# An attention and feed-forward block on one core: the front in written order, idle matmuls ahead of it, and the weights' check moved to SP's queue

## The chip, the cores and the metric

The kernel runs on one core of a Trainium2 chip. The metric is the device time of the whole kernel in microseconds (us); lower is better. Before the change the median of three runs is 1353.18 us.

The engines by the names of the profile: PE (TensorE, matmuls), DVE (VectorE), ACT (ScalarE), POOL (GpSimd) and SP (SyncE, which here only issues DMAs). ACT and POOL issue DMAs too.

## What is computed

The inputs are x of 4 x 1024 x 256 and weights. In short:

```python
x = x + layernorm(attention(layernorm(x), Wqkv, Wout))   # 16 heads of 16
x = x + layernorm(ffn(layernorm(x)))
# attention: softmax(q k^T / 4) v, then @ Wout.T
#            softmax is exp(x - max) / (sum + 1e-6)
# ffn:  h = silu(x w1 * s1) * (x w2 * s2)
#       h = gelu(h h1 * t1);  h = gelu(h h2 * t2);  h w3 * s3
```

The feed-forward weights are ternary in these inputs. The kernel computes with them in a rounded format, and counts on the chip whether any weight changes by the rounding (a second condition bounds the scores). Only if a count is not zero does a slow general branch run; with these inputs it doesn't.

## The kernel before

**Attention.** The four batches (`b`) have 16 heads in four groups of four (`g`), and the 1024 queries are taken in two halves (`h`). A *unit* is one (b, g, h), 32 in all, in that order. In a unit, eight chunks of 128 keys and two pairs of heads make 16 *tiles*. Per tile, `exponentials` (lines 434 to 442) makes two score matmuls into one of three PSUM buffers `s` and one exponential on ACT, 128 x 1024, into a ring of eight tiles; `weigh` (444) makes four matmuls into the accumulator `acc`, of which there is one; `rise` (451) takes maxima on DVE (`top`). At the end of a unit, `unit_end` (583) copies `acc` to `o` on DVE and adds the division to the side work.

**Group operands.** Scores are made from `stacks`, in which four parts (high and low of keys and queries) lie below one another. `stack(b, g)` (409) fills them by 32 DMAs from the projected `cq` tiles, all on SP's queue. There are two sets, used by groups in turn; `unit_end` of the second half of group g issues the `stack` of group g + 2, or of the next batch.

**Side work.** The loop of lines 841 to 861 makes three tiles in a turn and ends a turn with `side.take()` (553). That runs the steps of several chains which are due: a step has a gap, counted in turns from the step before it in its chain, or from the turn in which the chain was added. Only one step with tensor work is taken in a turn. Projections for the next batch, V, the division, the output projection, the layer norms and the score bound (`flags`) run this way.

**The weights' check.** `check_weights` (227) makes four steps for one of 22 blocks of 512 KB: `load` the block from memory to `w`, `cast` it on POOL to the rounded `wr`, and twice `count` on DVE, which compares half a block; the second count also stores `wr` back to memory, from where the feed-forward stage loads its weights. The tiles `w` and `wr` have one buffer each. In before, the load and the store are issued by POOL, and all 22 blocks are one chain in the side work (830), a block in five turns.

**The front.** What stands ahead of line 808 is ordered by a scheduler; within `tc.manual_schedule()` (808) every engine issues in the order in which the code is written. In the front, x of batch 0 is loaded by SP in four DMAs, the query and key weights (`slotted`, 1 MB) by ACT in one DMA, from which POOL copies `wqk_sb`. Then, half by half: layer norm on DVE with a power on POOL (`rstd`), transposes on PE, key and query projections (310) with a copy on ACT and a low part on DVE, and 16 copies per projection for group 0, alternately on SP and POOL. Two of the four V steps (300) precede the first scores; the other two are side work.

Of the kernel before, what the change touches and what calls it, by code (L numbers as in the profile page):

```python
# [9 lines left out]
F32 = mybir.dt.float32  # L10
# [8 lines left out]
P = 128  # L19
HEADS = 16  # L20
DH = 16
SLOT = 32
# [4 lines left out]
RING = 8  # L27
TURN = 3
# [2 lines left out]
SAFE = 25.0  # L31
FULL = 32.0
EARLY = 256
SPREAD = 32.0
NQ = 512
WIDE = 1024
# [77 lines left out]
def tile_fast(ctx: ExitStack, tc: tile.TileContext, x, wqk, wv, wo, w1, w1s, w2, w2s, h1, h1s, h2, h2s, w3, w3s, out, bad):  # L114
# [22 lines left out]
        t, n = NH + (TPQ - 1) * h, TPQ * h  # L137
        return (slice(n, n + 1), view[:, h : h + 1, :]), (slice(n + 1, n + TPQ), view[:, t : t + TPQ - 1, :])

    def load_x(b):  # L140
        view = x[b].rearrange("(t p) d -> p t d", p=P)
        for h in range(NH):
            for at, tokens in pieces(h, view):
                nc.sync.dma_start(out=xs[b][:, at, :], in_=tokens)

    load_x(0)
    ident = const.tile([P, P], F32, name="ident")
    make_identity(nc, ident)
    ones = const.tile([P, 1], F32, name="ones")
# [16 lines left out]
        nc.sync.dma_start(out=scales[name], in_=w)  # L166
    w3s_sb = const.tile([P, D], F32, name="w3s_sb")
    nc.sync.dma_start(out=w3s_sb, in_=w3s.partition_broadcast(P))


    keep = ctx.enter_context(tc.tile_pool(name="keep", bufs=1))
# [6 lines left out]
    with ExitStack() as actx, ExitStack() as rctx:  # L178
# [4 lines left out]
        wo_sb = aw.tile([P, DC, D], F32, name="wo_sb")  # L183
        with tc.tile_pool(name="load", bufs=1, side="right") as load:
            slotted = load.tile([P, DC, 2, HEADS, SLOT], F32, name="slotted")
            nc.scalar.dma_start(out=slotted, in_=wqk.rearrange("(c p) (k h s) -> p c k h s", p=P, k=2, s=SLOT))
            for c in range(DC):
                nc.gpsimd.tensor_copy(wqk_sb[:, c], slotted[:, c, :, :, 0:DH])
        nc.scalar.dma_start(out=wv_sb, in_=wv.rearrange("(c p) d -> p c d", p=P))

        def load_wo(c):
# [35 lines left out]
        def check_weights(n, c):  # L227

            k = blocks.index((n, c))
            st = {}  # L230

            def rows(w):
                return w[c * P : (c + rows_at_once[n]) * P, :].rearrange("(i p) d -> p i d", p=P)

            def load():
                st["w"] = work.tile([P, WIDE], F32, tag="w", name="w", bufs=1)
                nc.gpsimd.dma_start(out=st["w"].rearrange("p (i d) -> p i d", i=rows_at_once[n]), in_=rows(weights[n]))

            def cast():
                st["r"] = work.tile([P, WIDE], F32R, tag="wr", name="wr", bufs=1)  # L240
                nc.gpsimd.tensor_copy(st["r"], st["w"])

            def count(j):
                def run():
                    w, r = (t[:, NQ * j : NQ * (j + 1)] for t in (st["w"], st["r"]))
                    i = k * (WIDE // NQ) + j
                    nc.vector.scalar_tensor_tensor(w, w, 1.0, r.bitcast(F32), ALU.mult, ALU.not_equal, accum_out=misses[:, i : i + 1])
                    if NQ * (j + 1) == WIDE:
                        nc.gpsimd.dma_start(out=rows(rounded[n]).bitcast(F32), in_=st["r"].bitcast(F32).rearrange("p (i d) -> p i d", i=rows_at_once[n]))

                return run

            return [Step(load, 0, False), Step(cast, 3, False)] + [Step(count(j), 1, False) for j in range(WIDE // NQ)]

        def to_scalar(o, i, scale=1.0):
            nc.scalar.activation(o, i, AF.Copy, scale=scale)  # L256
# [137 lines left out]
        def copies(g, w, c0=0, c1=S):  # L394

            m, i = g // GPT, g % 2

            def copy(u, j, n):
                def run(queue):
                    k = "hi" if (j // 2 == 0 if w == 0 else j % 2 == 0) else "lo"  # L400
                    r = (g % GPT) * HPG * DH + (2 * u + n) * DH
                    o = n * ROWS + j * DH
                    queue.dma_start(out=stacks[w, i, u][o : o + DH, c0:c1].bitcast(F32), in_=cq[w, m, k][r : r + DH, c0:c1].bitcast(F32))

                return run

            return [copy(u, j, n) for u in range(2) for j in range(PARTS) for n in range(2)]
# [7 lines left out]
        def slots(b, g, t0=0, t1=NT):  # L415


            def run():
                nc.gpsimd.tensor_copy(
                    vaug[g % 2][:, t0:t1, :, 0:DH], cv[:, t0:t1, HPG * DH * g : HPG * DH * (g + 1)].rearrange("p t (h e) -> p t h e", e=DH)  # L420
                )
                slotted[g % 2] = b, g, t1

            return run
# [143 lines left out]
                    self.take()  # L568

        side = Side()  # L570
        accs, tops, ends, later = {}, {}, {}, {}

        def begin(b):

# [8 lines left out]
        def unit_end(b, g, h):  # L583

            o = both.tile([P, NQ], F32, tag="o", name="o", bufs=2)
            to_vector(o, accs[b, g, h])

            assert g or not b or not any(step.tensor for step in ends[b - 1, h][0])
            unit = side.add(divide(g, h, o, tops[b, g, h]), True)
            if g == NG - 1:  # L590
                unit[0].extend(ending(b, h, to_scalar if (b, h) == (B - 1, NH - 1) else to_vector))
                ends[b, h] = unit
            if h < NH - 1:
                return

            n, at = g + 2, b
            if n >= NG:
                n, at = n - NG, b + 1
            if b == B - 1 and g == NG - 2:
                load_weights("h1", range(HC // 2))  # L600
            if at < B:
                if at > b:
                    assert not later["chain"][0]
                stack(at, n)
                slots(at, n)()
            if g == NG - 3 and b + 1 < B:
                v, qk1 = later["rest"]
                assert not later["chain"][0]
                later["chain"][0].extend(v)
                side.add([Step(lambda: None, 5, False)] + qk1)  # L610
            elif g == NG - 3:
                side.add([Step(lambda n=n: load_weights(n), 1, False) for n in ("w1", "w2", "w3")])
                side.add([Step(lambda: None, 7, False)] + prepare(0, to_vector))
            if g == NG - 1:
                begin(b + 1)
# [189 lines left out]
                chain = side.add(finish(n, ffn["a"]), True)  # L805
            side.flush()

        with tc.manual_schedule():
            norm, xt, qk, v, flags = prologue(0, lambda n: ps.tile([P, 2, NQ], F32, tag="big", name=n)[:, 0, :], to_scalar)
            queues = [nc.sync, nc.gpsimd]  # L810
            for h in range(NH):
                for step in norm[h]:
                    step.run()
            for h in range(NH):
                for step in xt[h]:
                    step.run()
                for w, step in zip((1, 0), qk[0][h]):
                    step.run()
                    for i, copy in enumerate(copies(0, w, h * NQ, (h + 1) * NQ)):
                        copy(queues[i % len(queues)])  # L820
            stacked[0] = 0, 0
            for step in v[: len(v) // 2]:
                step.run()
            slots(0, 0, 0, NT // 2)()
            stack(0, 1)
            for c in range(DC):
                load_wo(c)
            side.add(v[len(v) // 2 :] + [Step(slots(0, 0), 0, False), Step(slots(0, 1), 0, False)] + sum(qk[1], []) + [Step(lambda: side.add(flags), 0, False)])
            begin(0)
            side.add([s for k in blocks for s in check_weights(*k)])  # L830
            made = seen = weighed = 0

            def make(end):

                nonlocal made
                for k in range(made, min(end, len(tiles))):
                    assert k - weighed < RING
                    exponentials(k)
                    made = k + 1

            while weighed < len(tiles):
                n = made
                make(n + TURN - side.borrowed)
                if made == len(tiles):
                    n = made
                for k in range(seen, n - 1, 2):
                    rise(k)
                    seen += 2
                while weighed + 2 <= n:
                    b, g, h, c, _ = tiles[weighed]  # L850
                    if c == 0:
                        accs[b, g, h] = ps_acc.tile([P, NQ], F32, tag="acc", name="acc")
                    weigh(weighed, accs[b, g, h])
                    weighed += 2
                    if c == NT - 1:
                        unit_end(b, g, h)
                        if n < len(tiles):
                            break
                make(n + TURN)
                if weighed < len(tiles):  # L860
                    side.take()

            load_weights("h1", range(HC // 2, HC))
            rctx.close()
            ffn["a"] = halves(ctx.enter_context(tc.tile_pool(name="fa", bufs=1, reuse_waits="tile")), "ha")
            feed_forward()


@with_exitstack
# [233 lines left out]
```

## Time and profile before

| what | value |
|---|---|
| median of three runs | 1353.18 us (1352.37 to 1354.74) |
| the profiled execution: its time, its span | 1352.66 us, 1350.9 us |
| mean granted TensorE clock | 0.991 |
| PE first works at | 12.33 us |
| first scores, first exponential at | 31.16 us, 31.75 us |
| one copy of `stack` on SP | 0.59 us issue, 2.3 us to landing |
| load of a weight block from POOL | 4.2 us to landing |
| cast of a block on POOL, half a count on DVE | 1.04 us, 0.68 us |

The span runs from the first to the last instruction that the profiler saw. A row of a timeline gives the start, the duration, the engine and line, the operation, output and input, and in brackets how long the engine was idle before it and what released it. An engine with a q (SPq) is that engine's instruction queue, as when it issues a DMA. The attention stage lasts to about 680 us; the feed-forward stage follows.

### The profile page before, as it was taken

To read this page: it belongs to the slowest core of one execution; us is meant where nothing else is said; L and a number is where in the kernel's file an instruction comes from. 1 tells how busy PE (TensorE), PEld (TensorE's weight loads), DVE (VectorE), ACT (ScalarE), POOL (GpSimd) and SP (SyncE) were. 2 spreads that over 40 slices of the span, in tenths; PEclk is the share of its full clock that TensorE was granted. 3 is DMA by queue.
4 is the path that set the end of the run, shared out by engine and by line. 5 is a ranking of instruction groups with operands and counts; after the bars stand their busy time and mean duration, and the time that the engine had idled before them with its cause. 6 is when DMAs were issued, how large, how long until landed. Compare 5 with 4: busy or idle time off the path is not lost.

```text
span 1350.9 us, 18751 instructions
## 1 busy us (share of the span) xinstructions
PE 1273.3 (94%) x7034; PEld 799.0 (59%) x7034; DVE 732.5 (54%) x1553; ACT 684.1 (51%) x820; POOL 159.7 (12%) x200
## 2 busy tenths in 40 slices
PE   5989999899899999989999999999999999999995
PEld 3333434343343433333478888888888888888884
DVE  3466568755697565735573452725436364363533
ACT  2677787676777678888842231413224141231410
POOL 6241133210421012000000000000000000000000
PEclk9989999899999999999999999999999999999998
DMA  7554344542445432336130000000000000000000
GB/s 215 130 113 110 80 111 91 141 103 60 129 108 133 94 51 48 50 65 195 54 134 1 1 16 0 17 1 0 16 1 16 0 14 3 0 16 0 17 0 19
DMA packets 38390, 79.62 MB, mean 59 GB/s; under 512 B 11280, under 2 KB 21136, under 8 KB 38288
## 3 DMA queue, kind: packets, MB, share of 16 engines
q1 hardware_dynamic: 30384, 52.88, 18.1%
q0 software_dynamic: 7360, 24.12, 5.3%
q10 hardware_dynamic: 544, 1.31, 0.3%
q8 instruction: 58, 0.95, 0.3%
q14 instruction: 44, 0.36, 0.1%
HBM read 28.98 MB, written 15.73 MB: 33 GB/s over the span
## 4 chain that ended last, share of the span: by engine, by line
PE 76%; DVE 12%; ACT 7%; issue 2%; POOL 1%; DMA 1%; SPq 1%; ACTq 0%; POOLq 0%; DVEq 0%
PE ph L686 35%; PE acc L449 13%; PE s L441 8%; ACT e L442 5%; PE p L314 5%; PE pz L739 4%; PE pg L686 3%; PE py L506 2%; PE pv L305 2%; DVE top L458 2%; DVE sg L702 2%; PE po L470 1%; DVE st L92 1%; DVE ha_lo L691 1%; DVE o L259 1%
## 5 line engine op out<-in xcount | busy, mean ns | idle before, releaser
L442 ACT ACTIVATE e<-s 128x1024 f32<-128x1024 f32 x512 | 484.9, 1032 | 143.4 <-PE s L441 128.0
L449 PE MATMUL acc<-e,vaug 128*32 128x512 f32 x2048 | 258.0, 607 | 0.1
L722 ACT ACTIVATE a<-ph,h_scale 128x512 f32<-128x512 f32 x128 | 81.0, 685 | 307.3 <-PE ph L686 307.3
L441 PE MATMUL s<-sq,sk 64*128 64x512 f32 x1024 | 195.9, 452 | 28.0 <-ACT e L442 20.3
L686 PE MATMUL ph<-hb_lo,h 128*128 128x512 f32 x512 | 199.7, 390 | 0.0
L686 PE MATMUL ph<-hb_hi,h 128*128 128x512 f32 x512 | 199.6, 390 | 0.0
L441 PEld LDWEIGHTS s<-sq,sk 64*128 64x128 f32 x1024 | 87.5, 185 | 164.5 <-ACT e L442 121.0
L458 DVE TENSOR_TENSOR top<-top,e 128x512 f32<-128x512 f32 x192 | 146.4, 762 | 29.7 <-ACT e L442 23.4
L102 POOL TENSOR_TENSOR rstd<-ve,minus_half 128x4 f32<-128x4 f32 (+1 forms) x33 | 37.1, 1125 | 772.5 <-DVE ve L100 772.5
L723 DVE CAST ha_hi<-a 128x512 fp32r<-128x512 f32 x64 | 27.1, 424 | 158.2 <-ACT a L722 158.2
L449 PEld LDWEIGHTS acc<-e,vaug 128*32 128x32 f32 x2048 | 49.7, 109 | 106.1 <-issue 96.7
L686 PEld LDWEIGHTS ph<-hb_hi,h 128*128 128x128 f32 x512 | 96.2, 188 | 20.1
L686 PEld LDWEIGHTS ph<-hb_lo,h 128*128 128x128 f32 x512 | 96.2, 188 | 20.0
L686 PE MATMUL ph<-ha_hi,sq 128*128 128x512 f32 x256 | 102.0, 399 | 0.4
L686 PE MATMUL ph<-ha_lo,sq 128*128 128x512 f32 x256 | 100.0, 391 | 0.0
L686 PE MATMUL ph<-ha_lo,sk 128*128 128x512 f32 x256 | 99.9, 390 | 0.0
L686 PE MATMUL ph<-ha_hi,sk 128*128 128x512 f32 x256 | 99.9, 390 | 0.0
L702 DVE SCALAR_TENSOR_TENSOR sg<-pg,w_scale,sg 128x512 f32<-128x512 f32 x64 | 47.1, 746 | 47.9 <-ACT sg L700 47.8
L700 ACT ACTIVATE sg<-pg,w_scale 128x512 f32<-128x512 f32 x64 | 43.3, 688 | 56.7 <-DVE ha_lo L691 47.4
L723 DVE CAST hb_hi<-a 128x512 fp32r<-128x512 f32 x64 | 27.0, 422 | 82.2 <-ACT a L722 82.2
L314 PE MATMUL p<-xT,wqk_sb 128*128 128x512 f32 x128 | 65.1, 635 | 0.2 <-ACT xT L256 0.2
L686 PEld LDWEIGHTS ph<-ha_hi,sq 128*128 128x128 f32 x256 | 48.2, 188 | 12.7 <-DVE sg L702 3.3
(144 smaller groups left out, 1679.6 us busy)
## 6 DMA issues: line engine op xcount, KB each, us to landing
w<-in_h_dram POOLq DMA_DIRECT2D x16, 512.0 KB, 4.4
h_r<-wr POOLq DMA_DIRECT2D x16, 512.0 KB, 3.6
sk<-ck1hi SPq DMA_DIRECT2D x64, 64.0 KB, 2.3
sk<-ck1lo SPq DMA_DIRECT2D x64, 64.0 KB, 2.3
sq<-cq1hi SPq DMA_DIRECT2D x64, 64.0 KB, 2.3
sq<-cq1lo SPq DMA_DIRECT2D x64, 64.0 KB, 2.3
h<-h_r SPq DMA_DIRECT2D x8, 512.0 KB, 7.1
sk<-ck0hi SPq DMA_DIRECT2D x56, 64.0 KB, 2.3
```

The lines of the kernel that those rows point to most:

```text
L102: nc.gpsimd.tensor_tensor(rstd[:, :n], ve[:, :n], self.minus_half[:, :n], ALU.pow)
L314: nc.tensor.matmul(pp, wqk_sb[:, c, w, HPT * m : HPT * (m + 1), :], st["xT"][:, c, h * NQ : (h + 1) * NQ], start=c == 0, stop=c == DC - 1)
L441: nc.tensor.matmul(s[:, a, :], stacks[1, g % 2, u][r, c * P : (c + 1) * P], stacks[0, g % 2, u][r, h * NQ : (h + 1) * NQ], start=True, sto ...
L442: nc.scalar.activation(pair(k)[:, u], s, AF.Exp)
L449: nc.tensor.matmul(acc[SLOT * i : SLOT * (i + 1), :], vaug[g % 2][:, c, i, :], pair(k)[:, i // 2, i % 2, :], start=c == 0, stop=c == NT - 1)
L458: nc.vector.tensor_max(top, top if c > 1 else pair(k - 2)[:, :, :, 0:P], pair(k)[:, :, :, 0:P])
L686: nc.tensor.matmul(p, homes[n][c][:, m * P : (m + 1) * P], half[:, c, :], start=c == 0 and k == 0, stop=c == len(homes[n]) - 1 and k == 1)
L700: nc.scalar.activation(sg, p[:, 0, :], AF.Silu, scale=scales["w1"][:, m : m + 1])
L702: nc.vector.scalar_tensor_tensor(sg, p[:, 1, :], scales["w2"][:, m : m + 1], sg, ALU.mult, ALU.mult)
L722: nc.scalar.activation(a, p[:, j, :], AF.Gelu, scale=scales[n][:, m : m + 1])
L723: nc.vector.tensor_copy(o[0][:, m, :], a)
L739: nc.tensor.matmul(p[t], half[:, c, t * P : (t + 1) * P], homes["w3"][c], start=c == 0 and k == 0, stop=c == HC - 1 and k == 1)
```

## The change

- `manual_schedule` now covers the front from the first load of x on, so every engine issues there in written order.
- The first DMAs: only the first half of x ahead of the scales, the second half after them; `slotted` in two DMAs of half the size; `wqk_sb` copied from it by ACT instead of POOL.
- `WARM` = 8 matmuls on PE, of `ident` and the zeroed `vaug`, whose result is not used, stand ahead of the first transposes.
- Layer norm of the second half is spread around the first half's.
- The 16 copies per projection go to three queues: two on ACT, seven each on SP and POOL.
- One V step instead of two precedes the first scores; three are side work.
- The check's load and store are issued by SP. The 22 blocks are no longer one chain: each unit end issues the load of one block and adds its other steps; the cast has a gap of 4 instead of 3.

```diff
+WARM = 8
...
-    load_x(0)
+    ctx.enter_context(tc.manual_schedule())
+    load_x(0, [0])
...
     nc.sync.dma_start(out=w3s_sb, in_=w3s.partition_broadcast(P))
+    load_x(0, [1])
...
-            nc.scalar.dma_start(out=slotted, in_=wqk.rearrange("(c p) (k h s) -> p c k h s", p=P, k=2, s=SLOT))
+            view = wqk.rearrange("(c p) (k h s) -> p c k h s", p=P, k=2, s=SLOT)
             for c in range(DC):
-                nc.gpsimd.tensor_copy(wqk_sb[:, c], slotted[:, c, :, :, 0:DH])
+                nc.scalar.dma_start(out=slotted[:, c], in_=view[:, c])
+            for c in range(DC):
+                nc.scalar.copy(wqk_sb[:, c], slotted[:, c, :, :, 0:DH])
...
             def load():
-                nc.gpsimd.dma_start(out=st["w"]..., in_=rows(weights[n]))
+                nc.sync.dma_start(out=st["w"]..., in_=rows(weights[n]))
...
                     if NQ * (j + 1) == WIDE:
-                        nc.gpsimd.dma_start(out=rows(rounded[n])..., in_=st["r"]...)
+                        nc.sync.dma_start(out=rows(rounded[n])..., in_=st["r"]...)
...
-            return [Step(load, 0, False), Step(cast, 3, False)] + [Step(count(j), 1, False) for j in range(WIDE // NQ)]
+            return [Step(load, 0, False), Step(cast, 4, False)] + [Step(count(j), 1, False) for j in range(WIDE // NQ)]
...
         def unit_end(b, g, h):
...
+            if checks:
+                load, *steps = checks.pop(0)
+                load.run()
+                side.add(steps)
             unit = side.add(divide(g, h, o, tops[b, g, h]), True)
...
+        idle = misc("idle")
+        for _ in range(WARM):
+            nc.tensor.matmul(idle, ident, vaug[0].rearrange("p t h s -> p (t h s)")[:, 0:NQ], start=True, stop=True)
+
+        queues = [nc.scalar, nc.sync, nc.gpsimd, nc.sync, nc.gpsimd, nc.sync, nc.gpsimd, nc.sync]
+        queues += [nc.scalar, nc.gpsimd, nc.sync, nc.gpsimd, nc.sync, nc.gpsimd, nc.sync, nc.gpsimd]
+        for step in norm[0] + norm[1][0:1] + xt[0][0 : TPQ // 2] + norm[1][1:] + xt[0][TPQ // 2 :]:
+            step.run()
...
+                for copy, queue in zip(copies(0, w, h * NQ, (h + 1) * NQ), queues):
+                    copy(queue)
...
-            for step in v[: len(v) // 2]:
+        v[0].run()
+        stack(0, 1)
...
+        early = [v[1], Step(slots(0, 0, 0, NT // 2), 0, False)]
+        side.add(early + v[2:] + [Step(slots(0, 0), 0, False), ...])
         begin(0)
-            side.add([s for k in blocks for s in check_weights(*k)])
+        checks.extend(check_weights(*k) for k in blocks)
```

In `unit_end` the new lines stand ahead of the call of `stack`.

## The prediction

> **What bounds the kernel now.** I read the page first (busy shares, slices), then the timeline of the first 50 us, then the waits of the attention stage, and last the timelines of SP's queue and of VectorE there, because the change moves work to SP.
>
> The page, share of each engine and PE by slice:
>
> ```profile
> span 1350.9 us, 18751 instructions
> PE 1273.3 (94%) x7034; PEld 799.0 (59%) x7034; DVE 732.5 (54%) x1553; ACT 684.1 (51%) x820; POOL 159.7 (12%) x200
> PE   5989999899899999989999999999999999999995
> w_r<-wr POOLq DMA_DIRECT2D x6, 512.0 KB, 4.0
> ```
>
> TensorE is the bound nearly everywhere. Only the first slice (33.8 us) is half empty; that is all a better front can win. The last line is the store of a checked weight block, 4.0 us to landing (3.6 for h1 and h2).
>
> The timeline of the front (start, us, engine, line, operation):
>
> ```profile
> 7.31 0.43 DVE L92 BATCH_NORM_STATS2 st<-x 128x6 f32<-128x256 f32 x1 [3.22 <-DMA x<-in_x_dram]
> ...
> 11.86 1.38 DVE L110 TENSOR_SCALAR xn<-x,mv,rstd 128x256 f32<-128x256 f32 x4
> 12.33 2.30 PE L295 MATMUL pt<-ident,xn 128*128 128x128 f32 x8 [12.33 <-DVE xn L110]
> ...
> 14.53 5.82 PE L314 MATMUL p<-xT,wqk_sb 128*128 128x512 f32 x8
> ...
> 24.07 3.70 PE L314 MATMUL p<-xT,wqk_sb 128*128 128x512 f32 x8 [0.25 <-ACT xT L256]
> ...
> 27.61 3.62 PE L305 MATMUL pv<-wv_sb,xT 128*128 128x256 f32 x16
> ...
> 31.75 2.85 ACT L442 ACTIVATE e<-s 128x1024 f32<-128x1024 f32 x3
> ```
>
> TensorE first works at 12.33; the same eight records of a projection take 5.82 us at first and 3.70 later; the first exponential is at 31.75.
>
> SP's queue and VectorE around the end of the second unit (batch 0, group 0, second half), from two timelines:
>
> ```profile
> 73.51 1.15 SPq L403 DMA_DIRECT2D sk<-ck1hi  x2
> ...
> 94.18 2.48 SPq L403 DMA_DIRECT2D sq<-cq1lo  x4
> ```
>
> ```profile
> 83.40 0.69 DVE L259 TENSOR_SCALAR o<-acc 128x512 f32<-128x512 f32 x1 [2.19 <-PE acc L449]
> ...
> 88.82 0.68 DVE L458 TENSOR_TENSOR top<-top,e 128x512 f32<-128x512 f32 x1
> ...
> 96.50 0.68 DVE L247 SCALAR_TENSOR_TENSOR w<-w,wr 128x512 f32<-128x512 f32 x1
> ```
>
> A batch of 32 copies (one `stack`) holds SP from 73.51 to 96.66: 23 us, starting 10 us before the unit's end (`o` leaves the accumulator at 83.40), as the keys' last reader is done by then. The next batches take 21 to 22 us. Counting a weight block is a VectorE instruction in the middle of the `top` and `o` work.
>
> The waits of the attention stage, and two stretches of it by window:
>
> ```profile
> POOL w L237 <- DVE w L247: 160.0, 19, 18.2
> ...
> 70.00:80.00 10.00, 7.40 (x56) 2.63 (x48) 7.80 (x20) 8.50 (x10) 6.50 (x7) 1.00 0.36 60
> 80.00:90.00 10.00, 8.83 (x44) 3.35 (x44) 6.01 (x16) 3.88 (x4) 7.92 (x9) 0.66 0.77 187
> ```
>
> POOL stands 160 us at the block load, waiting for VectorE's count; nobody minds, POOL is 12% busy. The windows show the price of a gap on TensorE: it waited 2.67 us up to 80.67, and then the granted clock is 0.66 of 10 us, that is half speed for 6.8 us, 3.4 us lost.
>
> [...] records of 0.855 us from 14.53 to about 18.8, then 0.428. [...] SP stood 248.7 us in 16 waits at line 403 for scores. [...] here 0.62 us a copy on SP and 0.48 on POOL.
>
> **The front, part by part.** *Idle matmuls.* Eight 128x512 f32 matmuls are 16 records (four make eight in L314), 13.7 us at 0.855. If the clock rises after 4.3 us, they last 4.3 + 9.4/2 = 9.0 us. They need `ident` and the first `vaug`, by POOL's memsets (0.20, 0.29, 0.95, 0.15 from 0.73) at about 2.4, and end at 11.4[...]. *First copies.* Only half of x (512 KB) and the two halves of `slotted` come first; at the 370 GB/s of 3 to 7 us the first half of x lands by about 4.2, and VectorE has `xn` by about 10 even behind the gather of two later tiles. So the idle matmuls end last. Transposes at 11.4, first projection 1.3 later at 12.7 instead of 14.53, at full clock 8 x 0.428 = 3.4: done at 16.1 instead of 20.35. The second half keeps its spacing (7.4 us to 27.77 in before) and ends at 23.5. The wqk copies move to ScalarE, idle then (0.6 each); the two copies it issues per projection cost 0.4 each there. *Scores ahead of V.* One V step (8 records, 1.75) instead of two stands before the scores: 25.3; SP's seven copies x 0.62 per projection instead of eight land the queries at about 26. First exponential 26.1 instead of 31.75: 5.65 us. But the V step returns in the loop, where TensorE is the bound, for 1.99: the front is worth -3.7. Bounds: -5 (all of it), 0 (TensorE's gap before the second half, 1.73 in before and 2.0 here, drops the clock). *POOL* loses 44 DMA issues of 0.55 and the blocked loads. The gap at 78 to 80.67 began with the cast and VectorE's count behind the squares; such stalls are worth between 0 and -12, I take -3.
>
> **The check on SP's queue.** This decides. Per loop three tiles are made, 16 tiles a unit, so unit ends come 5, 5, 6, 5, 5, 6 ... side steps apart (3.91 us each: 22 blocks x 5 steps from 35.3 to 465.5). Block k is loaded at unit end k; cast comes at step 4 after it, the counts at 5 and 6, the store with the second count. Where the next unit end is only five steps off, load k+1 is issued before count 6 and store k after it. If that end closes a group (k even), the 32 copies of `stack` are issued between them. SP's order is then: load k+1, 32 copies, store k. Both `w` and `wr` have one buffer. So:
> - load k+1 waits for the second count of k, which VectorE reaches after `o` and the division: U + 4.5 (U is the unit's end; in before the division ends 3.6 after it). The copies wait behind it; they had started at U - 10.
> - load 0.5 and copies 22: store k goes out at U + 27.0 and lands, at 3.7, at U + 30.7.
> - cast k+1 must not overwrite `wr` before that, and takes 1.04: U + 31.7. It was due at about U + 13.
> - count k+1 is due on VectorE at step 5, about U + 17.7, and everything there is queued behind it: the `top` steps and the next `o`. `acc` has one buffer, so TensorE stops for `o`, and ScalarE when the ring of eight tiles is full. Count 0.69, two `top` 1.4: `o` at U + 33.8 instead of U + 20.9.
>
> That is 12.9 us an event, 12.5 after some catching up from full buffers. It hits k even with a gap of five: 0, 4, 6, 10, 12, 16, 18, seven times: +87.5. After each, TensorE has stood far over 2.67 us; half clock costs up to 3.4, of which I take half (VectorE's backlog binds part of the time): +12. The other blocks: for k even with a gap of six, store k precedes the copies; for k odd, store k goes out behind copies that end some 8 us before the next cast. Both are free. The stacks land by U + 29.5 and are first read some 35 after U: free, with 5 us of cover. Bounds of an event: copies from U + 2, 21 us, landing 2.9 give 8.5; a count reached at U + 7, 23 us and a landing of 5.3 with the full clock loss give 20.
>
> Sum against the profiled execution (1352.66 around a span of 1350.9; the median of the runs is 1353.18, 0.5 above): 1352.7 - 3.7 - 3 + 87.5 + 12 = 1445.5.
>
> **Rivals.** *The store is in time* (faster): if SP reached store k before the cast, say because the copies still start early at U - 10 and end at U + 13, the check costs nothing and only front and POOL count: 1352.7 - 6.7 = 1346. For it: POOL carried the same transfers at no cost, and SP is idle half of each 42 us. Against: the load that waits for the count stands ahead of the copies. It decides once store k is out by about U + 13. *A smaller stall* (slower): SP is late but VectorE runs some 8 us later than I place it, so about 4 us an event remain: 1346 + 28 = 1374. *The front gives its lead back* and the check is free: a gap before the second half drops the clock (3.4) or the copies' DMAs wait for x still in flight ([...] `w3s_sb` at 7.31 behind x at 7.29): about 1353.
>
> **How the numbers follow.** Stalls as worked out 0.80, smaller stall 0.06, store in time 0.11, nothing left 0.03. A measurement here tells 0.2% (2.7 us) from no change. So slower 0.86, faster 0.11, same 0.03. The time is that of the first case, 1445. Its range follows from the event's bounds, damped as not all seven will lie at one end: 1390 to 1485; taken down to 1380 for part of the smaller stall.
>
> **What would show it.** On VectorE, seven idle stretches of about 14 us ahead of line 247, released by the cast, and POOL's cast waiting for the store's DMA; TensorE idle some 12 us there and a granted clock near 0.5 after it. On SP the copies start after a unit's end, not 10 us before. In the front: first score near 25, projections at 0.428 from the start. It is wrong if the stores land before the casts are due, or if the waits fall on POOL alone.

## The result, and the profile after

The changed kernel takes 1450.47 us, median of four runs (1450.38 to 1451.05), beside 1352.78 us for the kernel before on the same chip. The ratio is 1.0721, with a 95% interval from 1.0702 to 1.0739: 97.7 us slower.

The page of the changed kernel: the span, the share of each engine, PE and its granted clock by slice (tenths), and two groups of instructions with the idle time ahead of them:

```profile
span 1448.5 us, 18803 instructions
PE 1295.1 (89%) x7050; PEld 807.6 (56%) x7050; DVE 734.3 (51%) x1553; ACT 686.3 (47%) x822; POOL 135.5 (9%) x150
PE   8977959689749957999899999999999999999996
PEclk9988989899879978999999999999999999999999
...
L473 PE MATMUL po<-ident,top 128*128 128x128 f32 x128 | 24.1, 319 | 100.5 <-DVE top L463 100.5
...
L252 DVE SCALAR_TENSOR_TENSOR w<-w,wr 128x512 f32<-128x512 f32 x44 | 32.7, 744 | 89.6 <-POOL wr L246 89.6
```

VectorE's busy time hardly moved, 732.5 us before and 734.3 now, and ScalarE's went from 684.1 to 686.3. TensorE's grew by 21.8 us: 10 us are the idle matmuls, and most of the rest is work at half clock, as shown below. So the 97.7 us are for the most part waits. The slices say where: PE's row has holes in the attention stage only (the last slice is the end of the span, as before), and the clock falls in the same slices. The two groups say who waits for whom: PE stands 100.5 us for VectorE's `top` (line 463), and VectorE stands 89.6 us in front of the count (252; 247 before) for POOL's cast (246).

In the kernel before, the same two waits were short (waits from 30 to 690 us: us in total, times, the longest):

```profile
PE po L468 <- DVE top L458: 7.2, 11, 1.8
...
DVE w L247 <- POOL wr L241: 3.7, 2, 1.9
```

The waits of the changed kernel from 24 to 700 us carry the chain one link further, and those of SP's queue up to 700 us show its beginning, the load that waits for the count:

```profile
POOL wr L246 <- DMA h_r<-wr: 164.2, 10, 27.6
...
PE po L473 <- DVE top L463: 100.5, 18, 18.1
...
DVE w L252 <- POOL wr L246: 89.6, 7, 16.1
...
POOL wr L246 <- DMA w_r<-wr: 72.8, 4, 26.7
```

```profile
SPq L242 <- DVE w L252: 246.1, 21, 24.4
```

The cast waits for the store of the block before, seven times so long that VectorE waits for it. The first of the seven, from the timelines (start, us, engine, line; the unit before it ended at 83.44):

```profile
88.54 0.68 DVE L252 SCALAR_TENSOR_TENSOR w<-w,wr 128x512 f32<-128x512 f32 x1
89.75 1.15 SPq L408 DMA_DIRECT2D sk<-ck1hi  x2
...
107.47 2.49 SPq L408 DMA_DIRECT2D sq<-cq1lo  x4
110.00 0.58 SPq L254 DMA_DIRECT2D w_r<-wr  x1
113.18 1.04 POOL L246 CAST wr<-w 128x1024 fp32r<-128x1024 f32 x1 [18.55 <-DMA w_r<-wr]
114.25 0.69 DVE L252 SCALAR_TENSOR_TENSOR w<-w,wr 128x512 f32<-128x512 f32 x1 [11.72 <-POOL wr L246]
...
116.27 0.68 DVE L264 TENSOR_SCALAR o<-acc 128x512 f32<-128x512 f32 x1
116.50 1.09 PE L473 MATMUL po<-ident,top 128*128 128x128 f32 x4 [11.39 <-DVE top L463]
...
119.27 1.94 ACT L447 ACTIVATE e<-s 128x1024 f32<-128x1024 f32 x2 [13.81 <-PE s L446]
```

Read it downward: the second count of one block, for which the next load waits on SP; the first copies of the `stack` behind that load, and the last ones; right behind them the store, 3.2 us later the cast, then the count, and only then the `o` that frees the accumulator. PE idles 11.4 us and ScalarE 13.8. The price of the gap in clock is seen in windows of 10 us over the same stretch (columns: length; busy of PE, PEld, DVE, ACT, POOL with instructions; granted clock; DMA share; GB/s):

```profile
100.00:110.00 10.00, 4.82 (x36) 1.48 (x34) 1.34 (x3) 5.45 (x6) 0.00 (x0) 0.86 0.62 102
110.00:120.00 10.00, 3.50 (x16) 2.27 (x20) 4.02 (x10) 0.73 (x1) 1.04 (x1) 0.50 0.20 64
120.00:130.00 10.00, 10.00 (x54) 3.09 (x46) 5.16 (x10) 6.36 (x8) 1.04 (x1) 0.95 0.43 159
```

A ladder of unit ends (the start of the copy `o<-acc` that closes a unit, read from the timelines of both kernels) gives each event its size. The seven units that hold an event:

| event | unit begins and ends, after (us) | its length after | before | more |
|---|---|---|---|---|
| 1 | 83.44, 116.27 | 32.83 | 19.63 | 13.2 |
| 2 | 184.59, 218.47 | 33.88 | 19.85 | 14.0 |
| 3 | 239.42, 270.64 | 31.22 | 19.40 | 11.8 |
| 4 | 337.72, 369.46 | 31.74 | 23.59 | 8.2 |
| 5 | 393.07, 427.28 | 34.21 | 17.95 | 16.3 |
| 6 | 487.16, 521.51 | 34.35 | 20.76 | 13.6 |
| 7 | 543.61, 574.82 | 31.21 | 21.40 | 9.8 |

They sum to 86.9 us. The other units together lost 16 us, and the last unit ends 102.9 us later (775.51 against 672.61). Of the 16 us, 13.0 lie in the seven units right behind the events. In these the granted clock is 0.86 to 0.93, where it was 1.00 in six of them before and 0.93 in one, and TensorE is busy 12.7 us longer: that is the price of half clock after the stalls. The feed-forward stage behind the attention stage issues the same matmuls; the last VectorE instruction ends 102.5 us later (1442.75 against 1340.22). From there to the end of the span it is 5.8 us now and 10.7 before, with nothing in it but the last store. That gives the 97.6 us between the two spans. Why this tail differs is not known, but it goes with the queue of the check's DMAs: 5.4 to 6.0 us in the five kernels here that issue the load from SP, 7.7 to 8.3 us in the eight with the new front and both DMAs on GpSimd (one trace each).

The front did what it was written to do in its parts and gained nothing in sum (timeline of the changed kernel):

```profile
2.48 9.99 PE L822 MATMUL idle<-vaug,ident 128*128 128x512 f32 x16 [2.48 <-POOL vaug L213]
...
11.35 0.43 DVE L93 BATCH_NORM_STATS2 st<-x 128x6 f32<-128x256 f32 x1 [1.40 <-DMA x<-in_x_dram]
11.93 1.38 DVE L111 TENSOR_SCALAR xn<-x,mv,rstd 128x256 f32<-128x256 f32 x4
...
14.45 3.70 PE L319 MATMUL p<-xT,wqk_sb 128*128 128x512 f32 x8 [0.32 <-ACT xT L261]
...
20.34 1.76 PE L300 MATMUL pt<-ident,xn 128*128 128x128 f32 x8 [2.20 <-DVE xn L111]
...
22.96 6.56 PE L319 MATMUL p<-xT,wqk_sb 128*128 128x512 f32 x8 [0.85 <-ACT xT L261]
...
31.18 0.73 PE L446 MATMUL s<-sq,sk 64*128 64x512 f32 x4
```

The first projections run at full pace from their start (3.70 us instead of 5.82), the second ones for the most part at half clock (6.56 instead of 3.70; the granted clock is 0.50 from 22 to 28 us). The first score stands at 31.18, where it was at 31.16.

### The profile page after: what moved, and what is told of

Same layout as the page of the kernel before. It is cut to its first block, busy times and chain, and to the rows that moved or that the text cites. A ratio compares the mean times of both kernels' runs of the same rounds, so it can differ in the third digit from the quotient of the medians.

```text
span 1448.5 us, 18803 instructions
## 1 busy us (share of the span) xinstructions
PE 1295.1 (89%) x7050; PEld 807.6 (56%) x7050; DVE 734.3 (51%) x1553; ACT 686.3 (47%) x822; POOL 135.5 (9%) x150
## 4 chain that ended last, share of the span: by engine, by line
PE 68%; DVE 12%; SPq 8%; ACT 5%; issue 3%; DMA 3%; POOL 1%; ACTq 0%; POOLq 0%; DVEq 0%
PE ph L696 32%; PE acc L454 11%; SPq L408 8%; PE s L446 7%; PE pz L749 4%; PE p L319 4%; ACT e L447 4%; PE pg L696 2%; DVE top L463 2%; PE py L511 2%; DVE sg L712 2%; PE pv L310 1%; PE po L475 1%; DVE st L93 1%; DVE ha_lo L701 1%
## 5 line engine op out<-in xcount | busy, mean ns | idle before, releaser
L454 PE MATMUL acc<-e,vaug 128*32 128x512 f32 x2048 | 262.2, 615 | 0.3 <-POOL vaug L424 0.3
L446 PE MATMUL s<-sq,sk 64*128 64x512 f32 x1024 | 199.1, 460 | 26.5 <-ACT e L447 20.5
L463 DVE TENSOR_TENSOR top<-top,e 128x512 f32<-128x512 f32 x192 | 144.0, 750 | 29.7 <-ACT e L447 24.2
L473 PE MATMUL po<-ident,top 128*128 128x128 f32 x128 | 24.1, 319 | 100.5 <-DVE top L463 100.5
L473 PEld LDWEIGHTS po<-ident,top 128*128 128x128 f32 x128 | 15.9, 160 | 127.3 <-issue 93.3
L252 DVE SCALAR_TENSOR_TENSOR w<-w,wr 128x512 f32<-128x512 f32 x44 | 32.7, 744 | 89.6 <-POOL wr L246 89.6
```

What stands on the lines that cost most here:

```text
L446: nc.tensor.matmul(s[:, a, :], stacks[1, g % 2, u][r, c * P : (c + 1) * P], stacks[0, g % 2, u][r, h * NQ : (h + 1) * NQ], start=True, sto ...
L454: nc.tensor.matmul(acc[SLOT * i : SLOT * (i + 1), :], vaug[g % 2][:, c, i, :], pair(k)[:, i // 2, i % 2, :], start=c == 0, stop=c == NT - 1)
L463: nc.vector.tensor_max(top, top if c > 1 else pair(k - 2)[:, :, :, 0:P], pair(k)[:, :, :, 0:P])
L473: nc.tensor.transpose(pm[:, i], top[:, i // 2, i % 2], ident)
```

## The experiments on the stall

The theory is the chain of the first event: the load waits on SP's queue for the second count, the 32 copies behind it, the store behind those, the one `wr` behind the store. Each of the first three kernels breaks one link; the fourth has the front without the moved check. They ran beside the kernel before at 1352.21 us.

**Three turns between load and cast, as before, the rest as changed.**

```diff
-            return [Step(load, 0, False), Step(cast, 4, False)] + ...
+            return [Step(load, 0, False), Step(cast, 3, False)] + ...
```

> The changed kernel with the cast's gap back at 3, so that the second count of block k and its store come one turn earlier and always precede the load of block k+1 and the 32 copies. Theory (store k stuck behind the copies holds VectorE): no long wait of VectorE for the cast is left, 1350 to 1358 us. Rival A (512 KB transfers on SP's queue cost in themselves, by holding up the group copies): still above 1400. Rival B (the front costs much of the loss): above 1380.

Measured: 1356.54 us, ratio 1.0032 (1.0023 to 1.0041). The wait in front of the count has all but gone (waits, 24 to 760 us):

```profile
DVE w L252 <- POOL wr L246: 5.8, 2, 2.9
```

With one turn less the second count comes ahead of the unit's end, and with it the store stands ahead of that end's load and copies. In the place of the first event the store went out at 72.69, as soon as the cast was done (a store on SP waits for the cast alone). The second count ran at 80.59, the next load went out at 82.06, the copies from 82.49, and the unit ended at 83.40. With its own chain, then, the move to SP's queue is not the 7%; it is the move together with the fourth turn.

**Only the store goes back to GpSimd's queue; load, chain and four turns as changed.**

```diff
-    nc.sync.dma_start(out=rows(rounded[n])..., in_=st["r"]...)
+    nc.gpsimd.dma_start(out=rows(rounded[n])..., in_=st["r"]...)
```

> The changed kernel, gap 4, with only the store issued by POOL again; the load stays on SP ahead of the copies and still waits for the count. Theory: the store lands some 8 us after the unit's end, before the cast is due, so the stalls go although the copies still start late: 1350 to 1360 us. Rival C (the load's wait in front of the copies makes the group operands late, and that is what TensorE waits for): stays above 1420.

Measured: 1358.89 us, ratio 1.0048 (1.0033 to 1.0063), and no wait of VectorE for the cast. SP still stood 175.6 us at the load for the count, and that cost little: of the links it is the store's place in the queue that decides.

**The load issued behind the 32 copies of its unit end.** Then the copies no longer wait for the count and the store is reached earlier.

```diff
             if checks:
                 load, *steps = checks.pop(0)
-                load.run()
                 side.add(steps)
...
                 stack(at, n)
+            if load:
+                load.run()
```

> The changed kernel, gap 4, with the load of block k+1 issued after the 32 copies of the unit's end instead of ahead of them. Theory: the copies start some 10 us before the unit's end as in the kernel before, and end 13 us after it; store k lands at about 17 us, the count is due at 17.7: stalls of 0 to 3 us each are left, 1353 to 1375 us. If the store behind the copies were enough without the waiting load, above 1420.

Measured: 1398.91 us, ratio 1.0346 (1.033 to 1.0362), above what I expected. The first event of this kernel (its unit began at 83.06) shows why half the stall stayed:

```profile
96.08 0.51 SPq L242 DMA_DIRECT2D w<-in_w_dram  x1
...
96.65 0.42 SPq L254 DMA_DIRECT2D w_r<-wr  x1
...
102.03 1.04 POOL L246 CAST wr<-w 128x1024 fp32r<-128x1024 f32 x1 [7.94 <-DMA w_r<-wr]
103.10 0.69 DVE L252 SCALAR_TENSOR_TENSOR w<-w,wr 128x512 f32<-128x512 f32 x1 [3.70 <-POOL wr L246]
```

The copies were through by 96, where the store was out only at 110 in the changed kernel. But here a load of 512 KB went out 0.6 us ahead of the store, and the cast that waited for the store began 5.4 us after it. The stores of this kernel land in a median of 5.2 us (the six of `w_r`) and 5.3 us (the 16 of `h_r`), where both medians are 3.1 in the changed kernel. That one has both cases: 5.4 us for the seven stores with a load 0.4 us ahead of them, 3.0 for the other 15, to which those of its events belong. I had counted the order on the queue and left the load's own transfer out.

**The front of the change, the check as before.**

```diff
-                nc.sync.dma_start(out=st["w"]..., in_=rows(weights[n]))
+                nc.gpsimd.dma_start(out=st["w"]..., in_=rows(weights[n]))
...
-                        nc.sync.dma_start(out=rows(rounded[n])..., in_=st["r"]...)
+                        nc.gpsimd.dma_start(out=rows(rounded[n])..., in_=st["r"]...)
...
-        checks.extend(check_weights(*k) for k in blocks)
+        side.add([s for k in blocks for s in check_weights(*k)])
```

and three turns again.

> The front of the change alone; the check is as before (one chain, load and store on POOL, gap 3). The prediction's step for the front: 1349 (-3.7), between 1347.5 and 1352.5. What the trace of the changed kernel suggests instead (first scores at 31.18 as before, but one V step more still to do, and half clock in the second half's projections): +2, so 1354 to 1356.

Measured: 1351.77 us, ratio 0.9994 (0.9985 to 1.0002): the whole loss is the check's, and the front is not told from no change. That holds for the sum. In the trace the last unit ends 2.2 us later than before (674.79 against 672.61), and the tail behind the last VectorE instruction is 2.8 us shorter (7.9 against 10.7).

Over these kernels the loss follows the time that VectorE stood for the cast:

| kernel | VectorE stood for the cast (us) | against before (us) |
|---|---|---|
| as changed | 89.6 | +97.7 |
| load behind the copies | 39.9 | +46.7 |
| three turns | 5.8 | +4.3 |
| store on GpSimd | 0 | +6.7 |

## What is left of the check when it doesn't stall

Two of these kernels still lose some 5 us. The check differs from before in three things: queue, chain of its own, fourth turn. Three more kernels fill in the combinations.

**Own chain and four turns, both DMAs on GpSimd.** (Load and store of the changed kernel with `nc.gpsimd`.)

> The change, with the check's loads and stores both issued by GpSimd's queue again; the check's own chain with its gap of four turns stays. Theory (the stall needs the store behind the 32 copies on SyncE's queue; the chain and its gap are harmless): no idle time of VectorE in front of the check's count, and 1350.5 to 1353.5 us, so that the 4 to 7 us that were left with only the gap or only the store changed belong to the load on SyncE's queue. Rival A (the gap of four costs by itself): over 1355 us. Rival B (those 4 to 7 us come from the chain, not from the load): 1356 to 1359 us with no wait for the cast.

Measured: 1365.09 us, ratio 1.0091 (1.0077 to 1.0105), against my expectation and on the side of its first rival. Its timeline at the flags of the first batch:

```profile
88.42 0.69 DVE L252 SCALAR_TENSOR_TENSOR w<-w,wr 128x512 f32<-128x512 f32 x1
...
89.67 0.62 POOL L242 DMA_DIRECT2D w<-in_w_dram  x1 [6.05 <-issue]
...
91.95 5.78 DVE L111 TENSOR_SCALAR xn<-x,mv,rstd 128x256 f32<-128x256 f32 x2 [2.23 <-POOL rstd L103]
...
95.51 1.03 POOL L333 TENSOR_TENSOR sq<-ck1hi 128x512 bf16<-128x512 f32 x1
...
97.65 0.68 DVE L356 TENSOR_REDUCE norm<-pn 128x4 f32<-128x512 f32 x1
...
98.39 0.80 PE L446 MATMUL s<-sq,sk 64*128 64x512 f32 x2 [5.59 <-DVE norm L356]
```

With four turns the second count falls behind the unit's end (84.09), at 88.42. GpSimd stands 6.05 us in front of the load, which goes out right behind the count, and `rstd` and the squares stand behind it. So VectorE gets `rstd` late, and its two `xn` then run beside GpSimd's four squares (92.51 to 96.54): 5.78 us for two records that take 0.73 in the kernel before. `norm` stands behind them on VectorE, and TensorE waits 5.59 us for `norm`. GpSimd is 12% busy in the kernel before; a share of that kind counts neither these 6.05 us nor what stands behind them.

**The same with three turns.**

> The change with three turns instead of four and both DMAs issued by GpSimd: the check's own chain alone. Theory (with four turns the second count comes at the end of the unit, and the load that waits for it held GpSimd's queue, the squares behind it and with them TensorE, which made the 1365 us): with three turns the count is a turn earlier, the load waits less on GpSimd's queue, and the time is 1351.5 to 1357 us. Rival (the chain itself costs, whatever its gap): 1360 us or more.

Measured: 1360.91 us, ratio 1.0070 (1.0055 to 1.0085), on the rival's side: the chain costs some 7 parts in 1000 by itself, and the fourth turn at most a little beside it, as the intervals of the two kernels overlap.

**The queue alone: the check in the common list with three turns, both DMAs on SP.**

> The front of the change, the check in the common list of side steps and with three turns between load and cast as before, but its loads and stores issued by SyncE: the move of the queue alone. Theory (the stall needs a store that stands in program order behind the 32 copies of the same unit end and is needed before them; the common list puts load and store at other turns than the unit's end): at most one or two of the seven stalls, 1352 to 1375 us. Rival (any check on SyncE's queue stalls behind the copies): several stalls, 1400 us or more.

Measured: 1373.59 us, ratio 1.0171 (1.0151 to 1.019), inside the theory's range. Its ladder has two late units: the first ends at 75.87 instead of 62.39, and the one that begins at 353.73 is 8.2 us longer than before. VectorE stood for the cast three times, 30.5 us. The theory had named the store; here it is the load that comes too late. The first wait, 17.8 us, is for the first block, whose load goes out only at 68.14, behind the 32 copies and the 16 loads of the output weights in SP's queue. In the second, 10.1 us, store and load both stand behind the copies (368.60 and 369.23), and the cast waits for the load. So the turn as such is not safe on SP's queue either; what counts is on which side of the copies the transfer stands.

| check's list and turns | DMAs on GpSimd | store alone on GpSimd | both on SP |
|---|---|---|---|
| common list, 3 | 0.9994 | | 1.0171 |
| own chain, 3 | 1.0070 | | 1.0032 |
| own chain, 4 | 1.0091 | 1.0048 | 1.0721 |

(ratios to the kernel before; all have the new front.) Read by column and row: with its own chain and three turns, SP's queue is better than GpSimd's by 4 parts in 1000, about 5 us (2.5 us of it may be the tail: 5.4 us against 7.9). Keeping load and store off GpSimd is thus worth something, but the own chain takes some 10 us at the same time (0.9994 to 1.0070 on GpSimd). One way in which it does, a load that holds GpSimd until the count, is seen in the trace with four turns. Where it costs with three turns is open.

## The experiments on the front

All keep the check as before (1351.77 us) and change the front alone.

**No idle matmuls** (`WARM = 0`).

> The front of the change with the check as before (1351.8 us), and without the eight idle matmuls. Theory (what the idle matmuls win in the first projections is real, and it is lost because the clock falls again in front of the second half): the first half's projections run 6.5 us instead of 3.7, everything behind them moves by some 2.8 us, the first score goes from 31.1 to 33 to 34 us, and the time is 2 to 3 us more than with them, 1353.5 to 1355. Rival (the query copies on SyncE's queue are the bound of the front, and the idle matmuls win nothing): the first score stays within 0.5 us of 31.1 and the time at 1351 to 1352.5.

Measured: 1352.15 us, ratio 0.9993 (0.9983 to 1.0002). The first projections took 4.70 us instead of 3.70, the second ones 5.40 instead of 6.54, and the first score came earlier, at 30.19, which neither the theory nor the rival had. With the idle matmuls the one half is 1.0 us faster and the other 1.1 slower.

**The second half's normalisation ahead of the first half's low parts on VectorE.**

```diff
-        for step in norm[0] + norm[1][0:1] + xt[0][0 : TPQ // 2] + norm[1][1:] + xt[0][TPQ // 2 :]:
+        for step in norm[0] + xt[0][0 : TPQ // 2] + norm[1] + xt[0][TPQ // 2 :] + xt[1][0 : TPQ // 2]:
...
-                for step in xt[h]:
+                for step in xt[h][TPQ // 2 :]:
```

> The front of the change with the check as before (1351.8 us), but on VectorE the second half's normalisation is put ahead of the first half's low parts, and the second half's first statistics behind the first half's normalisation. Theory (the wait for xn at 19.5 us cools the clock): xn of the second half is done before 17 us, its transposes follow the first projections with less than 1 us between, its projections take 3.7 us instead of 6.5, and the first score comes at 28.5 to 30 us, then held by the copies of the query on SyncE's queue; the time is 1 to 2.5 us less, 1349.3 to 1350.8. Rival A (the copies were the bound anyway): projections in 3.7 us, but the first score at 30.5 or later and the time within 0.7 us of 1351.8. Rival B (a lead in the front is given back in the loop): first score 1 us or more earlier, time within 0.7 us of 1351.8.

Measured: 1352.79 us, ratio 0.9998 (0.9989 to 1.0008), no gain. The transposes did follow at once (16.86), and still the second projections began at 22.42 and took 6.49 us. ScalarE's timeline names the next link:

```profile
17.28 0.60 ACT L261 ACTIVATE cq0hi<-p 128x512 fp32r<-128x512 f32 x1 [1.34 <-PE pt L300]
19.42 2.31 ACTq L408 DMA_DIRECT2D sq<-cq0hi  x2
21.77 1.08 ACT L261 ACTIVATE xT<-pt 128x512 f32<-128x512 f32 x2 [3.90 <-DMA x<-in_x_dram]
```

The copy of `xT` stands on ScalarE behind the two query copies that ScalarE issues, and those were held until 21.7 by transfers of x.

**The same without idle matmuls.**

> The last kernel without the idle matmuls. If they only bring forward a clock that PE would reach by itself a little later: the first half's projections take 5 to 6.5 us instead of 3.7, the second half's 3.7 as there is no gap, the first score comes 1 to 3 us later than with them, and the time is 1 to 3 us more. If the copies on SyncE's queue are the bound, both are within 0.7 us of the kernel with them.

Measured: 1352.88 us, ratio 1.0004 (0.9996 to 1.0012); first score 30.50. Nothing for the idle matmuls here either.

**No copies on ScalarE** (the first queue of both lists is `nc.gpsimd`, on top of the early normalisation).

> The kernel with the second half's normalisation put early (1352.8 us), and the two first copies in each list of queues issued by GpSimd instead of ScalarE. Theory (ScalarE's query copies waited from 17.9 to 21.7 us and held the second half's xT behind them): xT is copied at 18 to 18.6 us, the second half's projections follow the transposes and run 3.7 us, the first score comes at 28 to 30 us, now held by the last query copies of SyncE or GpSimd; the time is 0.5 to 2.5 us less than 1352.8. Rival (a lead of the front is given back in the first units): the first score is at least 1 us earlier than 30.6, but the end of the first unit (62 us) and the time move by less than 0.7 us.

Measured: 1351.91 us, ratio 0.9998 (0.999 to 1.0007). Now the front runs as it was meant to, both projections at 3.70 us, the first score 4.6 us earlier, and the time stays, as the rival had it. Its timeline:

```profile
17.93 3.70 PE L319 MATMUL p<-xT,wqk_sb 128*128 128x512 f32 x8 [0.28 <-ACT xT L261]
...
26.47 0.69 PE L446 MATMUL s<-sq,sk 64*128 64x512 f32 x2 [3.11 <-DMA sq<-cq0lo]
...
30.44 3.78 PE L310 MATMUL pv<-wv_sb,xT 128*128 128x256 f32 x8
...
35.64 0.41 POOL L424 COPY vaug<-cv 128x256 f32<-128x256 f32 x1
...
36.10 1.06 PE L454 MATMUL acc<-e,vaug 128*32 128x512 f32 x8 [0.69 <-POOL vaug L424]
```

TensorE waits 3.11 us for the query copies, its next V step runs at about half its pace (3.78 instead of 1.99), and the first `acc` waits for `vaug`, which stands on GpSimd behind that queue's copies.

**Three V steps ahead of the scores, in that gap of 3.11 us.**

```diff
-        v[0].run()
+        for step in v[0:3]:
+            step.run()
```

(and the side work begins with `v[3]`)

> The kernel without ScalarE's copies (1351.9 us), with three V steps ahead of the scores instead of one, put into the stretch of 3.1 us in which TensorE waited for the query copies and after which its next V step ran 3.78 us instead of 1.99. Theory (in the first unit TensorE is the bound, so that work moved from the loop into this gap shortens the unit): the first score stays near 27 us, no V step runs at half clock, the first unit ends at 58 to 60.5 us instead of 62.3, and if that is kept the time is 1 to 4 us less, 1348 to 1351. Rival (the loop's first units are paced by what is not on TensorE, and a lead is given back up to the second unit): first unit earlier, time within 0.7 us of 1351.9.

Measured: 1352.65 us, ratio 1.0005 (0.9997 to 1.0013). The V steps ran at full pace (5.34 us for three) and the first score was at 27.53, but the first unit ended at 64.52, later than in theory and rival, and the wait moved on:

```profile
36.34 1.93 PE L454 MATMUL acc<-e,vaug 128*32 128x512 f32 x8 [3.85 <-POOL vaug L424]
```

| front | first score | first `acc` | first unit ends | second unit ends | ratio |
|---|---|---|---|---|---|
| before | 31.16 | 35.94 | 62.68 | 83.40 | |
| of the change | 31.11 | 36.16 | 62.39 | 83.96 | 0.9994 |
| no idle matmuls | 30.19 | 35.52 | 61.76 | 83.34 | 0.9993 |
| early normalisation | 30.57 | 35.61 | 61.85 | 83.42 | 0.9998 |
| both | 30.50 | 35.56 | 61.83 | 83.41 | 1.0004 |
| early, no copies on ScalarE | 26.47 | 36.10 | 62.33 | 83.90 | 0.9998 |
| and three V steps | 27.53 | 36.34 | 64.52 | 84.19 | 1.0005 |

A first score 4.6 us earlier than in the front of the change ends the first unit 0.06 us earlier. The column of the first `acc` says why: the accumulation starts between 35.5 and 36.3 us in all seven, and in the five new fronts with one V step ahead of the scores the unit ends 26.2 to 26.3 us behind it. Where the first score moved by 0.5 to 0.9 us, `acc` and both unit ends moved by 0.5 to 0.6 with it, too little for the time to show. Where it moved by 4.6, the lead went ahead of `acc`: into waits of the next scores for query copies (0.42 and 0.98 us), the V step of 3.78 us, and the wait for `vaug`. With three V steps ahead, V is there early, and `acc` still waits 3.85 us, as GpSimd copies `vaug` only at 35.87, behind the DMAs that it issues one after another. So the first unit waits for `vaug` and not for the first score alone. That an earlier `vaug` would shorten the time was not tested. No version beat the kernel before by more than can be measured.

## Why the prediction was right, and where it was not

**The stall** was right in its mechanism, its number and its size. The seven events are at the seven blocks that the prediction had named, and the copies start 6.3 us after the unit's end, not 10 us ahead of it. The prediction put the store at U + 27.0, its landing at U + 30.7, the cast's end at U + 31.7 and `o` at U + 33.8. The first event, with U = 83.44, has them at U + 26.6, U + 29.7, U + 30.8 and U + 32.8. Seven events were to cost 87.5 us, and the ladder has 86.9. Its bounds for one event were 8.5 to 20, and the seven measure 8.2 to 16.3, the smallest just below. The main step rested on VectorE keeping to its order over a long wait. That was an assumption of mine, as the two waits for the cast in the kernel before, 3.7 us in all, are too short to show it. In the changed kernel it did: VectorE stood up to 16.1 us at one count, and in the first event it ran `top` and `o`, at 114.87 and 116.27, only behind the count of 114.25, at which it had stood 11.72 us.

**The clock after the gaps** was taken at +12, and that was right too: the units behind the events lost 13.0 us at a granted clock of 0.86 to 0.93. The other 3 of the 16 us outside the events are not assigned.

**The front, -3.7**, is the step that failed, in its size. The front alone measures 0.9994, -0.4 us with an interval that includes no change. The terms:
- Idle matmuls to end at 11.4: they ended at 12.47, as their pace doubled later: their weight loads come every 0.86 us up to 7.76 and every 0.43 from 8.45, 6.0 us after the first matmul, where 4.3 was assumed.
- `xn` by about 10: it came at 11.93 (its start). The statistics of two tiles of the second half were put ahead of it and waited for their x until 11.35. The prediction had let x land in time "even behind the gather of two later tiles".
- "The second half keeps its spacing": it didn't, 6.56 us instead of 3.70. The prediction had this as its bound at 0 (the gap of 2.0 us drops the clock); it should have been the value. The gap was 2.20 us, and the clock 0.50 behind it.
- That copies can be held by x in flight stood in the third rival. What I didn't see is that copies held on ScalarE hold `xT` behind them, shown by the early normalisation (3.90 us).
- The larger error is behind all of them: that each us of the first score is a us of the time. Moving it 4.6 us moved the time by nothing, as the lead was lost again ahead of the first `acc`.

**POOL, -3**: the effect is there, about 5 us between the two queues with the own chain and three turns, but the own chain, which the prediction charged with nothing, takes more: some 10 us.

**The sum.** 1445.5 was predicted and 1450.5 measured. The events are 0.6 us less than predicted and the clock behind them 1.0 more. The 6.7 us that front and GpSimd were to win are a loss of 3.0 us in the attention stage, which makes 9.7; the feed-forward stage gives 0.4 back. The tail, which the prediction did not have, is 4.9 us shorter. That the sum is off by only 5 us is thus in part luck; without the shorter tail it would be off by some 10 us, still inside the range.

**The rivals** fell as the prediction said they would: "the store is in time" needed the store out by about U + 13, and it was out at U + 26.6. With the store on GpSimd it is in time, and then the time is 1358.89, not 1346. "The front gives its lead back" was true of the front, by both of the causes that it named, with the check not free.

## What to carry to other kernels

Before moving a DMA to another queue, write down what that queue holds at that turn, each waiting instruction ahead of it included, and then ask who needs the buffer that the DMA frees; with a single buffer, a late store stops a cast, a count and whatever the counting engine has queued behind it (in the first event here 18.55 us for the cast and 11.72 for the count). A step's due turn and its queue belong together: in a chain of its own, three turns on SP cost 4 us and four turns 98, and on GpSimd the same fourth turn hardly showed; in the common list three turns on SP cost 21. And before a front is made shorter, test whether its end is what the first loop waits for: a kernel with the first result early, read up to the next wait, answers it.

## What the runs showed of the hardware

- In two fronts TensorE was slower behind short gaps, in a third it wasn't. After a gap of 2.20 us in the front of the changed kernel the granted clock is 0.96 from 21 to 22 us and 0.50 from 22 to 23, so it fell ahead of the next gap, of 0.85 us; eight projection records then took 6.56 us instead of 3.70. After gaps of 3.11, 0.42 and 0.98 us in the front without copies on ScalarE a V step took 3.78 us instead of 1.99. A gap of 1.74 us at the same place of the kernel before, ahead of 22.08, cost nothing: the clock stayed at 1.00, and eight projection records took 3.70 us.
- In the changed kernel a store of 512 KB landed in a median of 3.0 us with no load just ahead of it, and of 5.4 us with a load of the same size issued 0.4 us ahead of it on the same queue.
- One `xn` of 128x256 on VectorE took 4.74 us, from 91.95, while GpSimd worked on four squares (92.51 to 96.54), and ended 0.15 us after the last of them; another `xn` of the same kernel, at 98.85, took 0.40. The trace doesn't show what held it.
- ScalarE issued its copies in its own instruction order: in the front with the early normalisation it did nothing else for 3.90 us while they were held.
